# One buffer for the normalized tokens of two sublayers, and two more blocks counted in the first

## The chip, the core and the metric

The kernel runs on one core of a Trainium2 chip. The core has five engines with their own instruction queues: PE (matrix products; its weight loads are listed as PEld), DVE (vector), ACT (scalar functions and copies), POOL (here mostly indirect transfers) and SP (here only starts transfers). Each engine works through its own queue in order and waits on semaphores for the others. The metric is the device time of one execution in microseconds, and the median of several runs.

## The reference, cut to what matters

The program is a network of four layers on 1250 tokens of 512 numbers, with a graph of 21,250 edges. The change lies between the first layer's second half and the second layer's first half:

```python
# layer 0, second half: experts chosen with balanced gates
xn = _layernorm(x)
gates = clip(xn @ gate_w, 1e-10)          # 1250 x 8, then 8 rounds of balancing
#   each round: divide each column by its sum, then each row by its sum
# each of 8 experts takes its N // 8 = 156 tokens of largest gate; a taken token
# whose gate is above 0.5 gets tok @ experts[e], the others get zero from e;
# a token's result is the sum over its experts / (number of experts that took it + 1)
x = x + moe(xn)

# layer 1, first half: graph attention beside a global attention, same input
xn = _layernorm(x)
x = x + gat(xn, src, dst) + mix(xn)
#   mix: q, k, v = xn @ Wq.T, xn @ Wk.T, xn @ Wv.T ; softmax of q over features,
#        of k over tokens; (q (k^T v) + xn) @ W1.T @ W2.T + the same
#   gat: two dense-graph attention layers of 4 heads; needs, for every pair of
#        nodes, how many edges join them
```

The last comment is why the kernel has a table of counts: 1250 x 1250 numbers that say how often an edge runs from one node to another. It depends on the edges alone, so it can be made at any time before layer 1's graph attention.

## The kernel before, in words

**Tiles.** The tokens lie in 10 tiles of 128 rows (the last has 98). `self.x` holds them all. `norm_tile(t, out)` (lines 215 to 223) writes the normalized rows of tile t, from a mean and a variance that `row_stats` made (lines 201 to 208: two statistics instructions and a sum on DVE, a square root on ACT); if `ready(t)` has been called before, only a reciprocal (line 221) and one DVE instruction (line 222) are left. `transpose_tile` (line 156) turns a 128 x 512 tile with four PE instructions (line 160) into a PSUM bank and copies it out with `evac`, which takes ACT (line 134) and DVE (line 136) in turn. `layernorm` (line 225) does both for all ten tiles.

**Counting.** `count_blocks(blocks, signs)` (line 666) is a generator. The edges are sorted by target and cut into 12 blocks of 107 nodes, each of 16 tiles of 128 edges (the last has 12). For every tile of edges it makes a one-hot row (`ohs`, 128 x 1251), multiplies it on PE with the targets' one-hot (`ohb`, loaded by SP at line 688) in three products of 512, 512 and 227 columns (line 711), and yields. The three sums of a block take three banks of PSUM, named `more`, of which there are just three. At the block's end they are emptied, brought together (`acc`) and stored to the table (lines 712 to 726; the two stores of line 1096). With `signs` the rows are signs made by ACT (line 695), and, once `count_even` is set, every second one is made by DVE (line 692); the differences of neighbouring columns are then taken on DVE (line 720) after ACT has emptied the banks (line 719). Without `signs` DVE makes true one-hots (line 697) and ACT alone empties the banks (line 725). The 128 x 1251 row of column numbers, `wide`, is made by POOL (line 675), and `at`, the edges' numbers, by DVE (line 678), once for each use of the generator.

**Layer 0's second half**, `layer0_ffn` (line 1629), with the counting of the first six blocks mixed in by calls of `self.count(n)`, each of which draws n tiles of edges:

- norms and turns of the ten tiles, and the gate products (line 171, 8 columns each)
- 8 balancing rounds (lines 1651 to 1664), a chain of one PE product and seven short DVE instructions each, with one counted tile a round
- the top choice: 20 rounds of `max` and `match_replace` on DVE (lines 1679 and 1683), with two counted tiles a round
- places and slots (lines 1687 to 1732), which end in `putI`, the row that each token goes to, and `getI`, the row that it is fetched from; PE turns the slots at line 1707
- 20 scatters on POOL (line 239) of the normalized rows to the experts' input, then 24 counted tiles
- the scattered rows are loaded (`xr`, line 1744), turned (`rT`), multiplied with the eight experts' weights (line 179, 160 columns) and the results turned back and stored (lines 1756 and 1759)
- for each tile: two gathers on POOL (line 231), two sums into `x` on DVE (line 1787), the statistics, and two counted tiles

**Layer 1's first half**, `layer1_attn` (line 2164): it opens its own pools for the normalized tokens (`xn`, natural, and `xnT`, turned), for weights and for PSUM, calls `layernorm`, and then `global_attention` (line 1790), which is given a second use of the counting generator, for the other six blocks, as `steps`: every step draws four counted tiles, and there is one step after each of the 12 key products and after each of the 10 turns of the keys (line 1817), and so on until the blocks are done. Then `gat_dense` uses the table.

**What sets the order.** The program text gives an order, but a scheduler, working at build time from the dependencies and from an estimate of each instruction's time, decides where each instruction stands in its engine's queue. Buffers come from pools: when a pool is closed and another one takes its place, the new buffers wait for the last users of the old ones. The chip then runs the queues as they are.

The functions that the change touches:

## Time and profile before

| | us |
|---|---|
| median of 3 runs | 4508.17 |
| lowest and highest | 4505.29, 4512.73 |
| the profiled execution's own time | 4474.11 |
| its span, first to last instruction | 4472.3 |

The stretches of the profiled execution that the change touches, in microseconds from the span's start:

| stretch | from | to |
|---|---|---|
| layer 0: norms, turns, gate | 1573.9 | 1601.5 |
| balancing | 1601.5 | 1621.2 |
| top choice, up to the turn of the slots | 1621.2 | 1705.1 |
| scatters, up to the first turn of the scattered rows | 1705.1 | 1740.3 |
| experts | 1740.3 | 1788.5 |
| gathers and sums | 1788.5 | 1826.0 |
| layer 1: norms, first key products | 1826.0 | 1843.8 |
| keys and counting | 1843.8 | 1916.9 |

A profile is one execution. The page's first part gives each engine's busy time, its share of the span and its number of instructions. The table of stretches gives for each window: its length, then the busy time and the number of instructions for PE, PEld, DVE, ACT and POOL, then the clock that PE was granted (1.00 is full speed, 0.50 is half), the mean busy share of the transfer engines, and the GB/s that they moved. The timeline gives start, duration, engine, line, operation, what is written from what, shapes and a count, and in brackets how long the engine had been idle and what ended that. Neighbouring instructions of one kind are merged into one line. Products in 32-bit floats appear as two entries each in the timeline.

### The profile page before, as it was taken

The page shows a single profiled execution, that of the slowest core. Times are in us where ns is not written, and L with a number is a line of the kernel's source. Part 1 is how long each engine was busy: PE and PEld are TensorE (multiplying, and loading weights), DVE is VectorE, ACT ScalarE, POOL GpSimd, SP SyncE. Part 2 cuts the span into 40 slices and gives each one's busy share as a digit, 9 for nine tenths or more (in the row PEclk, how much of TensorE's full clock was granted, in tenths as well). Part 3 has the DMA queues.
Part 4 walks back from the last instruction along what each step waited for, and adds up shares of the span by engine and source line. Part 5 has one row for each costly group of instructions (what it writes and reads, how often), then busy time and mean ns, then how long its engine had stood idle before and what let it go on. Part 6 is the DMA issues. An engine that isn't in the chain of part 4 may idle for free.

```text
span 4472.3 us, 49493 instructions
## 1 busy us (share of the span) xinstructions
PE 3913.2 (87%) x15451; PEld 2422.1 (54%) x15466; DVE 2696.8 (60%) x6357; ACT 1598.2 (36%) x2955; POOL 1358.0 (30%) x1308
## 2 busy tenths in 40 slices
PE   6987998899888866799999999997979896898796
PEld 3444554555454445444788877564546562455474
DVE  5358894888499864633896768314484225687301
ACT  2222442334233373110464446223452232555121
POOL 2017773776477402202000000103131013675102
PEclk9989999999999978899999999999999998997798
DMA  6437664766466423402421110384002653666695
GB/s 220 159 82 220 200 196 146 208 197 192 147 198 184 128 69 108 124 14 64 147 70 40 49 35 29 143 289 137 12 27 76 225 198 122 179 204 203 226 338 187
DMA packets 283002, 647.59 MB, mean 145 GB/s; under 512 B 61673, under 2 KB 108905, under 8 KB 267322
## 3 DMA queue, kind: packets, MB, share of 16 engines
q1 hardware_dynamic: 169290, 357.13, 24.1%
q0 software_dynamic: 73088, 234.75, 18.2%
q10 hardware_dynamic: 40352, 52.44, 3.4%
q8 instruction: 127, 2.08, 0.2%
q14 instruction: 145, 1.19, 0.1%
HBM read 528.87 MB, written 120.65 MB: 145 GB/s over the span
## 4 chain that ended last, share of the span: by engine, by line
PE 31%; DVE 8%; DMA 5%; issue 4%; ACT 2%; POOL 2%; SPq 0%; POOLq 0%; ACTq 0%; DVEq 0%
PE more L2105 5%; PE mm L1968 4%; PE mm L179 3%; PE mm L171 3%; PE mm L3168 2%; PE mm L2357 2%; PE mm L2352 2%; PE more L2688 2%; DMA hs<-gcn_h,srcI 1%; PE mm L2688 1%; PE mm L2067 1%; DMA xe<-routed_in 1%; PE mm L776 1%; DVE junk L1996 1%; DVE e L2030 1%
## 5 line engine op out<-in xcount | busy, mean ns | idle before, releaser
L231 POOL DMA_INDIRECT xl<-xl,srcI x564 | 617.5, 1095 | 282.4 <-issue 134.6
L1353 PE MATMUL more<-xl,wT 128*128 128x512 f32 x1128 | 578.6, 600 | 13.5 <-ACT wT L1343 13.0
L1286 PE MATMUL mm<-hl,oh 121*128 121x512 f32 x564 | 418.1, 741 | 56.7 <-DVE s L1299 32.7
L1302 DVE SCALAR_TENSOR_TENSOR junk<-s,att 128x512 f32<-128x512 f32 x534 | 416.3, 780 | 6.8
L1299 DVE TENSOR_TENSOR s<-xl,mm 128x512 f32<-128x512 f32 x534 | 357.7, 679 | 79.0 <-PE mm L1287 64.4
L2105 PE MATMUL more<-hh,e 128*128 128x259 f32 x1600 | 383.7, 385 | 10.8 <-ACT o L2048 8.5
L2105 PEld LDWEIGHTS more<-hh,e 128*128 128x128 f32 x1600 | 295.1, 191 | 74.8 <-issue 16.0
L171 PE MATMUL mm<-w,xnT 128*128 128x512 f32 x640 | 306.0, 617 | 16.7 <-ACT xnT L2383 12.1
L231 POOL DMA_INDIRECT hs<-gcn_h,srcI x188 | 217.1, 1155 | 85.7 <-issue 24.9
L1353 PEld LDWEIGHTS more<-xl,wT 128*128 128x128 f32 x1128 | 195.7, 192 | 73.7 <-issue 27.8
L1287 PE MATMUL mm<-hl,oh 121*128 121x512 f32 x564 | 234.1, 415 | 0.0
L231 POOL DMA_INDIRECT g<-routed_out,getI x60 | 67.3, 1122 | 486.7 <-DMA routed_out<-o 414.9
L1286 PEld LDWEIGHTS mm<-hl,oh 121*128 121x128 f32 x564 | 110.4, 196 | 191.1 <-issue 89.2
L2025 ACT ACTIVATE e<-r,hh 128x512 f32<-128x512 f32 (+1 forms) x240 | 154.3, 646 | 132.3 <-PE more L2105 121.3
L171 PEld LDWEIGHTS mm<-w,xnT 128*128 128x128 f32 x640 | 122.9, 197 | 143.7 <-issue 124.6
L3006 PE MATMUL more<-hl,oh 128*128 128x512 f32 x376 | 160.8, 529 | 27.0 <-DVE oh L2970 11.6
L1273 ACT ACTIVATE oh<-nb 112x512 fp32r<-112x512 bf16 x141 | 88.7, 630 | 266.4 <-DMA nb<-nbt 197.4
L2028 ACT ACTIVATE e<-r,a 128x512 f32<-128x512 f32 (+1 forms) x240 | 152.3, 646 | 68.8 <-DVE e L2030 56.7
L1166 PE MATMUL tab<-w,xT 128*128 128x512 f32 x320 | 166.2, 614 | 8.9 <-ACT xT L1415 6.1
L2030 DVE TENSOR_TENSOR e<-e,e 128x512 f32<-128x512 f32 (+1 forms) x240 | 141.9, 597 | 51.6 <-ACT e L2025 45.3
L1287 PEld LDWEIGHTS mm<-hl,oh 121*128 121x128 f32 x564 | 111.1, 197 | 111.1 <-issue 109.5
L2966 ACT ACTIVATE hl<-hs,rec 128x512 fp32r<-128x512 f32 x188 | 131.0, 717 | 98.2 <-DMA hs<-gcn_h,srcI 45.7
(631 smaller groups left out, 7783.3 us busy)
## 6 DMA issues: line engine op xcount, KB each, us to landing
w<-L_ffn_Wp SPq DMA_DIRECT2D x64, 1024.0 KB
w<-L_ffn_table SPq DMA_DIRECT2D x56, 1025.0 KB
neg<-ntab SPq DMA_DIRECT2D x80, 320.0 KB
nb<-nbt SPq DMA_DIRECT2D x141, 128.0 KB
hl<-xr SPq DMA_DIRECT2D x36, 448.0 KB
xr<-tro SPq DMA_DIRECT2D x30, 512.0 KB
xe<-routed_in SPq DMA_DIRECT2D x56, 256.0 KB
routed_out<-o ACTq DMA_DIRECT2D x56, 256.0 KB
```

The source lines that it names most:

```text
L171: self.nc.tensor.matmul(p, lhsT=xT[:, c, t * 128:(t + 1) * 128], rhs=w[:, c, n0:n0 + n], start=c == 0, stop=c == k - 1)
L231: self.nc.gpsimd.indirect_dma_start(out=out, out_offset=None, in_=table, in_offset=bass.IndirectOffsetOnAxis(ap=idx, axis=0), bounds_check ...
L1166: nc.tensor.matmul(d[name], lhsT=xT(c), rhs=L[name][:, c, :], start=c == 0, stop=c == 3)
L1286: nc.tensor.matmul(m, lhsT=s, rhs=hl[:K, 0, :], start=True, stop=False)
L1287: nc.tensor.matmul(m, lhsT=s, rhs=hl[:K, 1, :], start=False, stop=not on_pe(i))
L1299: nc.vector.tensor_tensor(o, d["xl"][:, j, :D], s, op=ALU.add)
L1302: nc.vector.scalar_tensor_tensor(junk, s, 0.0, L["att"], op0=ALU.max, op1=ALU.mult, accum_out=d["lg"][:, j:j + 1])
L1353: nc.tensor.matmul(B[b]["y"], lhsT=d["wT"][:, j, :], rhs=d["xl"][:, j, :D], start=k == 0 and j == 0, stop=last and j == GE - 1)
L1968: nc.tensor.matmul(m, lhsT=chunk(layer, c)[:, t * 128:(t + 1) * 128], rhs=w[:, c, :], start=c == 0, stop=c == k - 1)
L2030: nc.vector.tensor_tensor(e1[:, :n], e1[:, :n], e2[:, :n], op=ALU.max)
L2105: nc.tensor.matmul(ys[j], lhsT=e[:, j * 128:(j + 1) * 128], rhs=HH[q][:, s, :], start=s == 0, stop=s == NT - 1)
L3006: nc.tensor.matmul(y, lhsT=oh, rhs=hl[:, i], start=i + j == 0 and not (self.fast and k), stop=last and i + j == GE)
```

## The change: what it does

- `CB`, the number of blocks counted with signs in layer 0, goes from 6 to 8; the second use of the generator counts the other 4.
- One function, `layer0_ffn_to_layer1_attn`, replaces the lines in `run` and `layer1_attn`. It opens one `xnT`, one `xn`, one pool of weights and one set of PSUM banks for both halves, and passes `xn` and `xnT` to `layer0_ffn`.
- In `layer0_ffn` each of layer 0's ten norm tiles draws one counted tile; the 24 after the scatters become 56; and in the gather loop each tile, as soon as its sums and statistics are done, is normalized and turned for layer 1 into the same `xn` and `xnT`, with one counted tile instead of two. The pool of short-lived tiles moves to the other side of the memory.
- What is left of the first eight blocks is drawn after `layer0_ffn`; then the counting buffers are closed and opened again for the second use, and `global_attention` follows without a `layernorm` of its own.

```diff
-CB = 6
+CB = 8
@@ run
-            self.count_ctx = ExitStack()
-            with self.weights():
-                self.count_pool = self.count_ctx.enter_context(
-                    self.tc.tile_pool(name="count", bufs=1, side="right"))
-                self.ctab = self.dram.tile([NP, NP], F16 if fast else F32, name="ctab")
-                self.counting = self.count_blocks(range(CB), True) if fast else iter(())
-                with self.psum(3, 2, 3) if fast else self.psum():
-                    self.layer0_ffn()
-                    for _ in self.counting:
-                        pass
-            self.count_ctx.close()
-            self.count_pool = self.count_ctx.enter_context(
-                self.tc.tile_pool(name="count", bufs=1, side="right"))
-            self.layer1_attn()
+            self.layer0_ffn_to_layer1_attn()
@@
+    def layer0_ffn_to_layer1_attn(self):
+        fast = self.fast
+        count_ctx = ExitStack()
+        def count_pool():
+            self.count_pool = count_ctx.enter_context(
+                self.tc.tile_pool(name="count", bufs=1, side="right"))
+        self.ctab = self.dram.tile([NP, NP], F16 if fast else F32, name="ctab")
+        with self.tc.tile_pool(name="l1a", bufs=1) as p:
+            xnT = p.tile([128, 4, NP], F32, name="xnT")
+            with self.tc.tile_pool(name="l1b", bufs=1) as pb:
+                xn = pb.tile([128, NT, D], F32, name="xn")
+                with self.weights(), self.psum(3, 2, 3) if fast else self.psum():
+                    count_pool()
+                    self.counting = self.count_blocks(range(CB), True) if fast else iter(())
+                    self.layer0_ffn(xn, xnT)
+                    self.count(NB * 16)
+                    count_ctx.close()
+                    count_pool()
+                    if fast:
+                        steps = islice(self.count_blocks(range(CB, NB), False), 3, None, 4)
+                    else:
+                        steps = self.count_steps()
+                    self.global_attention(xn, xnT, steps)
+                    for _ in steps:
+                        pass
+            count_ctx.close()
+            with self.psum(2, 2, 4), self.tc.tile_pool(name="l1g", bufs=1, side="right") as pg:
+                self.gat_dense(xnT, pg)
@@ layer0_ffn
-    def layer0_ffn(self):
+    def layer0_ffn(self, xn, xnT):
...
-                self.tc.tile_pool(name="l0ft", bufs=2) as tmp:
+                self.tc.tile_pool(name="l0ft", bufs=2, side="right") as tmp:
...
-            xn = p.tile([128, NT, D], F32, name="xn")
-            xnT = p.tile([128, 4, NP], F32, name="xnT")
-            self.layernorm(xn, xnT)
+            for t in range(NT):
+                self.norm_tile(t, xn[:, t, :])
+                self.transpose_tile(xnT[:, :, t * 128:(t + 1) * 128], xn[:, t, :])
+                self.count(1)
...
-            self.count(24)
+            self.count(56)
...
                 self.ready(t)
-                self.count(2)
+                self.norm_tile(t, xn[:, t, :])
+                self.transpose_tile(xnT[:, :, t * 128:(t + 1) * 128], xn[:, t, :])
+                self.count(1)
@@
-    def layer1_attn(self):
...
```

More of the change, by code (lines that the diff above doesn't have):

```diff
@@ L2162, in gat_dense @@
                 step[0] += 1
-    def layer1_attn(self):
-        nc, I = self.nc, self.I
-        with self.tc.tile_pool(name="l1a", bufs=1) as p:
-            xnT = p.tile([128, 4, NP], F32, name="xnT")
-            with self.weights(), self.psum(3, 2, 3) if self.fast else self.psum():
-                with self.tc.tile_pool(name="l1b", bufs=1) as pb:
-                    xn = pb.tile([128, NT, D], F32, name="xn")
-                    self.layernorm(xn, xnT)
-                    if self.fast:
-                        steps = islice(self.count_blocks(range(CB, NB), False), 3, None, 4)
-                    else:
-                        steps = self.count_steps()
-                    self.global_attention(xn, xnT, steps)
-                for _ in steps:
-                    pass
-            self.count_ctx.close()
-            with self.psum(2, 2, 4), self.tc.tile_pool(name="l1g", bufs=1, side="right") as pg:
-                self.gat_dense(xnT, pg)
     def top2(self, p, v):
```

## The prediction

> **What bounds the kernel now.** I read the page first, then one table of engine times over the eight stretches that the change touches, the same table for the counting products alone (line 711), and the timeline around the joints. The program is a series of stages, each with its own limit, so the 87% for PE says little:
>
> ```profile
> span 4472.3 us, 49493 instructions
> ...
> PE 3913.2 (87%) x15451; PEld 2422.1 (54%) x15466; DVE 2696.8 (60%) x6357; ACT 1598.2 (36%) x2955; POOL 1358.0 (30%) x1308
> ```
>
> The stretches, in order: norms and gate; balancing; top choice; scatter; experts; gathers; layer 1's norms; layer 1's keys and the turning of the keys.
>
> ```profile
> core 0: us, PE busy (x) PEld busy (x) DVE busy (x) ACT busy (x) POOL busy (x), PEclk, DMA share, GB/s
> 1573.90:1601.50 27.60, 26.49 (x122) 25.27 (x123) 10.11 (x31) 9.46 (x11) 1.00 (x1) 0.50 0.45 166
> 1601.50:1621.20 19.70, 12.25 (x51) 6.20 (x52) 12.43 (x57) 15.23 (x12) 0.00 (x0) 0.83 0.06 20
> 1621.20:1705.10 83.90, 52.16 (x198) 21.87 (x202) 80.28 (x95) 69.78 (x65) 0.00 (x0) 0.85 0.13 37
> 1705.10:1740.30 35.20, 14.64 (x67) 7.11 (x67) 11.38 (x32) 12.60 (x14) 22.68 (x21) 0.69 0.24 71
> 1740.30:1788.50 48.20, 46.84 (x336) 44.80 (x336) 12.11 (x26) 10.44 (x26) 0.00 (x0) 0.95 0.53 178
> 1788.50:1826.00 37.50, 7.68 (x41) 4.09 (x42) 27.38 (x58) 1.74 (x9) 23.06 (x20) 0.64 0.72 164
> 1826.00:1843.80 17.80, 15.89 (x56) 10.58 (x57) 11.33 (x34) 3.34 (x7) 0.00 (x0) 0.70 0.64 237
> 1843.80:1916.90 73.10, 72.08 (x336) 40.20 (x342) 48.07 (x97) 19.33 (x35) 0.00 (x0) 1.00 0.21 64
> ```
>
> PE is full in the first stretch, at half clock; DVE is full in the third; in the fourth PE is idle for 20.6 of 35.2 us while POOL issues 20 scatters; in the sixth it is idle for 29.8 us under the gathers; in the last it is full at full clock. So a counting product is free in the scatter stretch and costs its whole time in the last. The counting alone:
>
> ```profile
> 1573.90:1601.50 27.60, 0.99 (x2) 0.47 (x3) 0.50 0.45 166
> ...
> 1705.10:1740.30 35.20, 13.49 (x57) 5.98 (x57) 0.69 0.24 71
> ...
> 1843.80:1916.90 73.10, 42.68 (x215) 21.64 (x222) 1.00 0.21 64
> ```
>
> The timeline gives prices and joints:
>
> ```profile
> 1598.58 0.59 PE L711 MATMUL more<-ohs,ohb 128*128 128x512 bf16 x1
> 1599.39 0.40 PE L711 MATMUL more<-ohs,ohb 128*128 128x227 bf16 x1 [0.22 <-issue]
> 1740.32 1.97 PE L160 MATMUL tp<-ident,xr 128*128 128x128 f32 x8 [20.06 <-DMA xr<-l0moe_in]
> 1825.21 0.73 DVE L1787 SCALAR_TENSOR_TENSOR x<-g,G,x 98x512 f32<-98x512 f32 x1
> 1845.73 0.42 DVE L136 COPY big<-mm 128x256 f32<-128x256 f32 x1 [4.47 <-PE mm L179]
> 1868.58 2.28 PE L711 MATMUL more<-ohs,ohb 128*128 128x512 bf16 x12
> ```
>
> A counted tile is three products: 1598.58 to 1599.79 is 1.2 us at half clock; twelve in 2.28 us is 0.57 us a tile at full clock. PE waits 20 us for the scattered rows. The last sum of layer 0 ends at 1825.9; PE's first 256-column key product starts at 1843.8, so 17.9 us lie between.
>
> [...] The trace agrees for the norms (turns and 8-column gate products, half clock from 1573.9 until 1608), less so after 1740.3, where turns alone took the clock up within 5 us. [...] here a scatter took 2.12 us beside a subtraction of line 720 and mostly 0.98 without. [...]
>
> **The change part by part.** The order of instructions in the changed program, as built, tells where each counted tile goes on PE (before, then after): norms and gate 1, 11; balancing 12, 12.3; top choice up to the slots' turn 64, 62.3; scatter 19, 38.3; between experts and layer 1's norms 14, 4; from there to the first 256-column key product 0, 8; afterwards 78, 52. The total is 188 in both.
>
> 1. *Norms and gate, ten tiles more.* PE is full, so each is on the path. If the clock stays at half: 10 x 1.2 = 12 us. But the new order begins with 7 turns, a tile, a turn, a tile, 4 turns: over 5 us without a gap, mostly wide products, which should release the clock. At full clock the same work is cheaper: 8 turns take 1.97 us at half and 1.04 to 1.13 at full (1837.8, 1767.0); a weight load is 0.216 us against 0.137 (40 in 8.66 at 1590, 16 in 2.20 at 1750), so the 80 gate products fall from 17.1 to about 11. If the first 6 us are slow and the rest fast: 28 turns 3.7 + gate 11 + 9 tiles 5.1 = 19.8, ending at 1599.8. ACT, which makes the one-hots (1.24 to 1.34 us each, 11 and five copies of 0.59: some 18 us), is covered. Ends: -2 and +12. I take 0, because three wide products a tile are what the old stretch lacked. SP issues three ohb loads ahead of gw (some 1.7 us later); gw is now first read behind two tiles, which covers it.
>
> 2. *Balancing to the slots.* DVE is a serial chain here. One subtraction L720 (1.44) moves into the fifth balancing round, between lines 1662 and 1663; from there to putI there are 5 of them instead of 4, and 12 L692 in both: +1.4. The first three rounds took 2.63 us against 2.36 for the others; with the clock up before them -0.8. Sum +0.7; ends +0.3 and +2.5.
>
> 3. *Scatter.* 38.3 tiles instead of 19. Those 19 ran from 1706.3 to 1720.3: 5 tiles at half clock in 5.0 us, the rest at about 0.61 (one-hots by ACT and DVE in turn), and a stop while ACT empties the banks. For 36.6 tiles before the first turn of the scattered rows: 5 x 1 + 31.6 x 0.61 + 2 stops x 2.4 = 29 us, against 34 that PE has: hidden. On SP, xr's loads stand behind the seventh block's two stores and four ohb loads; that block ends at about 1725, the scatters at 1736.5. Without the cover each tile would cost 0.6. Ten more L692 and 1.7 tiles among xr's turns: +1; ends 0 and +6.
>
> 4. *Experts to gathers.* The four mix weights (1 MB each) move on SP from 1826 to where experts 4 to 7 leave their buffers (about 1769 to 1787). The last lies beside the last two output stores (0.25 MB each, 1788.4), for which the first gather waits: at the 390 GB/s that such loads reached at 1580 a megabyte is 2.7 us. I take +1; ends 0 and +3. In return PE doesn't wait for the key weights. The eighth block's last four tiles replace 14 behind the experts; both lie under the wait for the gathers.
>
> 5. *Norms among the gathers.* Removed: the norms, turns and copies in the 17.9 us after the last sum. Added per tile on DVE, beside 2 x 0.75 + 0.68 + 0.17 + 0.15: reciprocal 0.15, norm 0.54, half a copy 0.35. That is 3.5 us by durations, about 3.0 by spacing (two sums stood 0.67 apart at 1808.5). With four one-hots of 0.54, at's 0.33 and a copy, DVE needs 33 to 38 us; POOL needed 1796.3 - 1825.9 = 29.6 for the loop and gains the iota L675 (1.2 + 0.3) behind the 11th gather, which nine gathers queue behind. So the last norm ends at 1831 to 1834 instead of about 1837.5; then four turns (1.0), one product and four tiles (3.1 at full clock, 6.7 at half), and the 256-column product starts at about 1838.3: -5.5; ends -9 and 0.
>
> 6. *Layer 1.* 26 tiles fewer in a stretch where PE is full: 26 x 0.57 = -14.8. The cover of the exponential's chain (4.7 tiles at the first turns of the keys) is in the new order too, and the turns without a tile beside them now stand among the products of line 1827. I take -14.5; ends -15 and -12.
>
> Sum: 0 + 0.7 + 1 + 1 - 5.5 - 14.5 = -17.3 us. The profiled execution took 4474.1 (span 4472.3); changed, 4456.8. The runs' median is 4508.2, 34 above it; the same difference gives 4490.9. Later stages are the same instructions in the same order and shift whole.
>
> **The rivals.**
> *The norms stay at half clock* (for: turns and gate products kept it there for 34 us; against: the gapless start). Term 1 is +12, the sum -5.3: 4502.9.
> *DVE becomes the bound under the gathers* (for: 27.4 of 37.5 us busy already; against: the spacing). Term 5 is 0, the sum -11.8: 4496.4.
> *Slower: the clock stays at half in the norms and in the scatter stretch too.* Then 36.6 tiles at 1.25 with two stops are 50.5 us in 35.2: +15 in term 3, +12 in term 1; sum about +10: 4518. It decides once a scatter tile averages above 0.93 us (34 / 36.6) and the norms gain nothing; each tenth above is 3.7 us. Against: the clock was up from 1711.7 while tiles followed each other.
> *The change doesn't do what it says:* excluded for the order (norms stand among the sums, tiles moved); possible only as waits that keep PE standing.
>
> **How the numbers follow.** My forecast, 4491: 0.57, its own range 4482 to 4499. Cold norms, 4503: 0.22. DVE-bound gathers, 4496: 0.12. Slower, 4518: 0.09. A measurement of this kernel tells 0.2%, 9 us, from no change: faster is below 4499. The forecast gives nearly all of its share, the gathers most of theirs, cold norms a tenth: faster 0.66. Slower (above 4517) is half of its rival and a little for unseen waits, 0.07; same 0.27. For 8 in 10 the range goes from 4480 (term 5 at -9, term 4 at 0, term 1 at -2, term 6 at -15, so a sum near -26) to 4512 (cold norms, and half of the scatter's overrun).
>
> **What would show it.** First balancing product no later than 1602, with a clock above 0.5 in the norms (term 1); the scattered rows' first turn still about 35 us behind the slots' turns, PE idle just before it (3); the last x sum within 33 us of the first gather's landing, and the key products some 12 us behind it (5); counting in the key stretch down by a third and the stretch still full (6). It is wrong if the norms stretch by 10 us, if xr's loads are issued late, or if gathers come more than 1.7 us apart.

## The result and the profile after

The changed kernel takes 4489.8 us (median of 13 runs, 4480.1 to 4503.5) against 4503.7 for the kernel before in runs alongside (13 runs, 4487.6 to 4515.1): ratio 0.997, 95% interval 0.9956 to 0.9984. That is faster by 13.9 us between the medians, or 0.3%; the forecast was 17.3 us less, and 4491 for the time itself.

The profiled execution of the changed kernel took 4489.8 us, with this span and these totals on its page:

```profile
span 4487.9 us, 49486 instructions
...
PE 3922.2 (87%) x15466; PEld 2415.7 (54%) x15466; DVE 2689.5 (60%) x6338; ACT 1622.8 (36%) x2976; POOL 1351.0 (30%) x1308
```

This span is 15.6 us longer than the one profiled before, although the kernel is faster. The profile tells why that is no contradiction: the first turn of layer 0's norms comes 21.4 us later (1573.9 before, 1595.3 after), in stages that the change doesn't touch, and from the end of layer 1's products of P (those of line 1827, which follow the keys) to the end of the span it is 2518.7 us before and 2527.1 after, unchanged instructions again. Between these two points, where the change lies, it is 379.7 us before and 365.5 after: 14.2 less, which agrees with the medians. All that follows is therefore measured between such anchors inside one trace, not from the start of the span.

The table of engine times over the stretches, in the order and with the columns of the one shown before (norms and gate; balancing; top choice; scatter; experts; gathers; from the last sum to the first 256-column key product; keys):

```profile
core 0: us, PE busy (x) PEld busy (x) DVE busy (x) ACT busy (x) POOL busy (x), PEclk, DMA share, GB/s
1595.30:1618.00 22.70, 21.90 (x153) 17.50 (x153) 10.50 (x31) 20.12 (x21) 1.01 (x1) 0.85 0.60 208
1618.00:1637.70 19.70, 13.27 (x53) 6.72 (x53) 12.46 (x54) 15.97 (x16) 0.00 (x0) 0.74 0.12 35
1637.70:1722.30 84.60, 52.07 (x201) 21.46 (x198) 80.93 (x100) 71.38 (x66) 0.00 (x0) 0.81 0.13 38
1722.30:1762.10 39.80, 28.51 (x120) 13.41 (x121) 15.33 (x39) 24.89 (x24) 20.59 (x20) 0.75 0.28 86
1762.10:1809.50 47.40, 46.49 (x347) 44.17 (x346) 12.96 (x28) 12.78 (x28) 0.00 (x0) 1.00 0.73 235
1809.50:1853.40 43.90, 13.58 (x48) 7.39 (x46) 29.37 (x70) 4.42 (x14) 22.18 (x21) 0.62 0.75 170
1853.40:1864.90 11.50, 10.82 (x44) 5.30 (x42) 8.02 (x22) 2.06 (x5) 0.00 (x0) 0.80 0.05 13
1864.90:1938.00 73.10, 72.38 (x306) 38.71 (x305) 37.62 (x74) 17.42 (x31) 0.00 (x0) 1.00 0.16 50
```

The first row is the surprise: with ten tiles more PE is through five us sooner, at a mean clock of 0.85 instead of 0.50. The scatter row is 4.6 us longer than before, the gather row 6.4 us longer, and the row behind the last sum, 17.8 before, is 11.5. The counting products alone, in the norms, the scatter stage and the keys:

```profile
1595.30:1618.00 22.70, 8.72 (x33) 3.66 (x33) 0.85 0.60 208
1722.30:1762.10 39.80, 27.35 (x110) 12.18 (x110) 0.75 0.28 86
1864.90:1938.00 73.10, 30.91 (x158) 15.21 (x156) 1.00 0.16 50
```

The tiles are where the order said: 11 in the norms, 36.7 before the scattered rows' first turn, and 158 products instead of 215 in a key stretch that is still full.

Term by term, in us between the same anchors. Term 1 runs from the first norm turn to the first balancing product, 2 on to the slots' turns, 3 on to the first turn of the scattered rows, "experts" to their last turn, 4 on to the first gather, then some four us to the first x sum; 5 from there to the first 256-column key product, 6 on to the end of P's products. w1_pool, explained below, differs from the changed kernel in the queue of one load, which lies at the same place in time, and serves as a second look at it.

| term | before | changed | forecast of the difference | measured | w1_pool | measured |
|---|---|---|---|---|---|---|
| 1 norms and gate | 27.67 | 22.76 | 0 | -4.9 | 22.54 | -5.1 |
| 2 balancing to slots | 103.55 | 104.21 | +0.7 | +0.7 | 102.60 | -1.0 |
| 3 slots to scattered rows | 35.20 | 39.86 | +1 | +4.7 | 36.00 | +0.8 |
| experts | 47.67 | 46.67 | 0 | -1.0 | 48.65 | +1.0 |
| 4 experts to first gather | 4.21 | 7.02 | +1 | +2.8 | 10.52 | +6.3 |
| 5 first x sum to 256-column product | 47.54 | 44.99 | -5.5 | -2.6 | 45.22 | -2.3 |
| 6 keys to the end of P | 109.78 | 95.95 | -14.5 | -13.8 | 95.95 | -13.8 |
| all, with first gather to first sum | 379.68 | 365.53 | -17.3 | -14.2 | 365.28 | -14.4 |

The total is near the forecast because term 1, five us better than forecast, and terms 3 to 5, in sum eight us worse in either profile, were off in opposite directions. The experiments ask why.

### The profile page after: what moved, and what is told of

The parts are those of the page before. It is cut to its first block, busy times and chain, and to the rows that moved or that the text cites. A ratio compares the mean times of both kernels' runs of the same rounds, so it can differ in the third digit from the quotient of the medians.

```text
span 4487.9 us, 49486 instructions
## 1 busy us (share of the span) xinstructions
PE 3922.2 (87%) x15466; PEld 2415.7 (54%) x15466; DVE 2689.5 (60%) x6338; ACT 1622.8 (36%) x2976; POOL 1351.0 (30%) x1308
## 5 line engine op out<-in xcount | busy, mean ns | idle before, releaser
L1353 PE MATMUL more<-xl,wT 128*128 128x512 f32 x1128 | 579.7, 601 | 14.5 <-ACT wT L1343 14.0
L2129 PEld LDWEIGHTS more<-hh,e 128*128 128x128 f32 x1600 | 295.1, 191 | 75.8 <-issue 17.8
L711 PE MATMUL more<-ohs,ohb 128*128 128x512 bf16 x564 | 137.5, 383 | 42.8 <-ACT ohs L695 18.0
```

The lines of the kernel that those rows point to most:

```text
L1353: nc.tensor.matmul(B[b]["y"], lhsT=d["wT"][:, j, :], rhs=d["xl"][:, j, :D], start=k == 0 and j == 0, stop=last and j == GE - 1)
L2129: nc.tensor.matmul(ys[j], lhsT=e[:, j * 128:(j + 1) * 128], rhs=HH[q][:, s, :], start=s == 0, stop=s == NT - 1)
```

## The experiments

Twelve kernels were run. Times of the stretches are from each one's own trace, one execution each, between the same anchors; ratios are to the kernel before, run alongside. The ratios alone say little about single causes: the interval of every one of the twelve except struct6 overlaps the changed kernel's, so what follows rests on the traces, and on how far they agree with each other.

**norms_bare: what brings the clock up.**

```diff
             for t in range(NT):
                 self.norm_tile(t, xn[:, t, :])
                 self.transpose_tile(xnT[:, :, t * 128:(t + 1) * 128], xn[:, t, :])
-                self.count(1)
             gw = pg.tile([128, 4, 8], F32, name="gw")
```

> The changed kernel without the counted tile per normalized tile in layer 0's norms; ten tiles come later instead (four among the gathers, six behind them), nothing is left out. Clock theory: the tiles are what brings TensorE's clock up, so the norms and the gate, 22.8 us in the changed kernel, go back to 27 to 28 us at a granted clock near 0.5, although PE has ten tiles (30 products) less to do there; about 4.5 us longer. Rival, work alone: the clock would rise anyway, and the stretch gets shorter by ten tiles of 0.57 to 1.2 us, to 11 to 17 us. Behind the gathers six tiles of 0.57 us: 0 to 3.4 us longer. Whole kernel: theory 4 to 8 us slower than the changed one, 0.998 to 0.999 of before; rival 3 to 8 us faster.

Norms and gate took 27.68 us, against 27.67 in the kernel before; ratio 0.9978 (0.9967 to 0.9989). The same windows, the first six us and the rest, of the changed kernel and then of norms_bare:

```profile
1595.30:1601.30 6.00, 5.39 (x20) 3.44 (x21) 5.42 (x11) 4.79 (x6) 1.01 (x1) 0.50 0.88 289
1601.30:1618.00 16.70, 16.51 (x134) 14.06 (x134) 5.08 (x20) 15.33 (x16) 0.00 (x0) 0.98 0.50 179
```

```profile
1581.40:1587.40 6.00, 5.30 (x23) 4.50 (x24) 5.71 (x11) 1.37 (x3) 0.98 (x1) 0.50 0.94 303
1587.40:1609.00 21.60, 21.41 (x101) 20.76 (x101) 4.39 (x20) 8.08 (x8) 0.00 (x0) 0.50 0.34 128
```

Both begin equally busy (5.39 and 5.30 of 6 us). Then the changed kernel runs at 0.98 and norms_bare, 99% busy for 21.6 us, stays at 0.50. The clock theory holds, the rival of mere work falls by more than 10 us. The other traces agree: in all eleven that have tiles in the norms the recorded clock rises 5.2 to 7.3 us after the first turn, and in the three without them (the kernel before, norms_bare, struct6) it stays at 0.50 until the norms are over. Behind the last sum norms_bare has only one tile more than the changed kernel, the others stand mostly under the wait for the gathers, and terms 5 and 6 together took 139.85 against 140.94: there the tiles cost nothing.

**scat40: fewer tiles behind the scatters.**

```diff
             self.count_even = True
-            self.count(56)
+            self.count(40)
```

> The changed kernel with 40 counted tiles asked for behind the scatters instead of 56: sixteen tiles come later (four among the gathers, twelve behind them). Theory: the scattered rows' first turn was 4.7 us late because it stands behind 36.6 counted tiles on PE, which ran at 1.3 us a tile from the ninth us of the scatters on; with 16 fewer it starts 35.2 us behind the slots' turns again (39.9 in the changed kernel), and PE idles before it. Twelve tiles more behind the gathers cost 12 x 0.57 = 6.8 us, so the end comes 1 to 3 us later than in the changed kernel. Rival, the scatters or the loads of the scattered rows themselves are late: the first turn stays 39 to 40 us behind the slots, and the end comes 6 to 7 us later.

The first turn of the scattered rows came 36.15 us behind the slots' turns, ratio 0.997 (0.9958 to 0.9982). That looks like the theory, but it is a poor test: most of the tiles that were to leave run in the stage all the same (35.0 before that turn instead of 36.7), and kernels that leave the stage untouched gave the same: w1_pool 36.00, norms_behind 35.59, gated4 35.97. So the 39.9 of the changed kernel's profile is nothing that its order always brings. The counting in the scatter stage (PE alone), in the changed kernel's profile and then in w1_pool's:

```profile
1733.86 4.99 PE L711 MATMUL more<-ohs,ohb 128*128 128x512 bf16 x24 [0.69 <-ACT ohs L695]
1740.52 1.22 PE L711 MATMUL more<-ohs,ohb 128*128 128x512 bf16 x6 [1.67 <-issue]
1743.11 1.26 PE L711 MATMUL more<-ohs,ohb 128*128 128x512 bf16 x6 [1.37 <-ACT ohs L695]
1745.97 2.25 PE L711 MATMUL more<-ohs,ohb 128*128 128x512 bf16 x6 [1.60 <-ACT ohs L695]
1752.97 2.40 PE L711 MATMUL more<-ohs,ohb 128*128 128x512 bf16 x6 [4.75 <-issue]
1756.07 6.24 PE L711 MATMUL more<-ohs,ohb 128*128 128x512 bf16 x25 [0.69 <-ACT ohs L695]
1762.14 0.60 PE L160 MATMUL tp<-ident,xr 128*128 128x128 f32 x4
```

```profile
1723.12 8.59 PE L711 MATMUL more<-ohs,ohb 128*128 128x512 bf16 x42 [0.69 <-ACT ohs L695]
1732.19 1.27 PE L711 MATMUL more<-ohs,ohb 128*128 128x512 bf16 x6 [0.49 <-ACT half L719]
1734.15 5.29 PE L711 MATMUL more<-ohs,ohb 128*128 128x512 bf16 x25 [0.69 <-ACT ohs L695]
1748.36 1.11 PE L160 MATMUL tp<-ident,xr 128*128 128x128 f32 x4 [8.93 <-DMA xr<-l0moe_in]
```

In w1_pool the fourteen tiles of a block follow each other in 8.59 us (0.61 a tile, as the prediction had it), all are done at 1739.4, and PE idles for 8.9 us until the scattered rows land: the stage is hidden. In the changed kernel's profile the same tiles come in pairs with 1.4 to 4.8 us between them. There PE and the makers of one-hots wait for each other: ACT's and DVE's next one-hot starts when a signal from PE comes in, and these signals arrive 1 to 7 us behind the modelled end of the product they tell of (0.04 to 0.6 us in w1_pool). What is known of that is taken up at the end.

**w1_pool: one weight load on another queue.**

```diff
-            w1 = self.weight(I["L1_mix_W1"], 4, D)
+            w1 = self.weight(I["L1_mix_W1"], 4, D, nc.gpsimd)
```

> The changed kernel with one of the four mix weights (L1_mix_W1, 1 MB) loaded from POOL's queue, behind the gathers, instead of SP's queue beside layer 0's last two output stores. Theory: those stores took 5.1 and 5.3 us to land beside that load, 2.0 and 2.3 us in the kernel before, and the first gather waits for them; with the load gone from there they land in 2 to 2.5 us and the first gather starts 4.2 us behind the experts' last turn instead of 7.0. Rival, the eighth block's store to ctab is what the first gather waits for: it stays near 7 us. Another: POOL's own issue of the load delays a gather or the iota, and the x sums take 2 us longer. Whole: theory 2 to 3 us less than the changed kernel up to the end of the products of L1827's kind; rivals 0 or 2 more.

The first gather came 10.52 us behind the experts' last turn, not 4.2; ratio 0.9965 (0.9951 to 0.9978). The edit didn't do what it was to do: in the built order POOL issues the load ahead of the gathers, which wait, at 1796.3, and so beside the last two output stores (1797.4 and 1797.9) as before. These landed after 8.0 and 8.4 us, no sooner than with all four loads on SP (5.1 to 7.9 us in six traces with four buffers). Who issues the load brought nothing here. The question of term 4 stayed open until gated4.

**norms_behind: the norms out of the gather loop.**

```diff
                 self.ready(t)
-                self.norm_tile(t, xn[:, t, :])
-                self.transpose_tile(xnT[:, :, t * 128:(t + 1) * 128], xn[:, t, :])
                 self.count(1)
+            self.layernorm(xn, xnT)
             g1.close()
```

> The changed kernel with layer 1's norms and turns behind the whole gather loop again instead of tile by tile in it; buffers still shared, eight blocks, same counts. Theory, the norms among the gathers bring 2.6 us because DVE, slower in the loop, gives back half: from the first x sum to the first 256-column key product 47 to 48 us instead of 45.0; the x sums alone take about 30 us again instead of 33.5, and some 17 us follow. Rival one, the whole gain of that stretch is from the key weights being there early and the tiles moved, not the norms: 45 us or less. Rival two, predicted before: the norms among the gathers bring 5.5 us: 50 us or more.

From the first x sum to the first 256-column product it took 52.0 us, which was written down for rival two; ratio 0.9981 (0.9973 to 0.9989). So the norms among the gathers are worth 52.0 - 45.0 = 7.0 us, and not 2.6. The reason that the changed kernel shows only 2.6 of it against the kernel before is the tiles: eight counted tiles stand behind the last sum in the changed kernel and in norms_behind, none in the kernel before, and 47.5 + 8 x 0.57 = 52.1. The stretch behind the last sum of norms_behind, then the rest up to the end of P:

```profile
1837.20:1859.16 21.96, 19.90 (x80) 12.54 (x81) 14.73 (x42) 3.92 (x8) 0.00 (x0) 0.76 0.02 7
1859.16:1955.12 95.96, 95.23 (x359) 48.87 (x358) 38.34 (x75) 17.99 (x32) 0.00 (x0) 1.00 0.13 38
```

**struct6 and count8: the two halves of the change alone.** struct6 is the changed kernel with the old counting:

```diff
-CB = 8
+CB = 6
...
                 self.transpose_tile(xnT[:, :, t * 128:(t + 1) * 128], xn[:, t, :])
-                self.count(1)
             gw = pg.tile([128, 4, 8], F32, name="gw")
...
-            self.count(56)
+            self.count(24)
...
                 self.transpose_tile(xnT[:, :, t * 128:(t + 1) * 128], xn[:, t, :])
-                self.count(1)
+                self.count(2)
             g1.close()
```

> The shared buffers and the norms among the gathers alone: six blocks in layer 0 and the counts asked for as in the kernel before (none in the norms, 24 behind the scatters, two a tile in the gathers). Theory, the gain is the counting's and the structure only pays for itself: norms and gate 26 to 28 us at half clock again; the first gather some 9.5 us behind the experts' last turn (4.2 before), because the mix weights' loads lie beside the output stores; from the first x sum to the end of the products of P some 150 us, against 157.3 before and 141 in the changed kernel; in sum about 2 us less than before, ratio 0.999 to 1.001. Rival, the structure brings the larger part: 10 us or more less than before, ratio 0.998 or lower.

count8 is the kernel before with the new counting:

```diff
-CB = 6
+CB = 8
...
-            self.layernorm(xn, xnT)
+            for t in range(NT):
+                self.norm_tile(t, xn[:, t, :])
+                self.transpose_tile(xnT[:, :, t * 128:(t + 1) * 128], xn[:, t, :])
+                self.count(1)
...
-            self.count(24)
+            self.count(56)
...
                 self.ready(t)
-                self.count(2)
+                self.count(1)
```

> The counting alone: the kernel before (own buffers, layer 1's norms behind the gathers) with eight blocks in layer 0 and the changed kernel's counts (one a tile in the norms, 56 behind the scatters, one a tile in the gathers). Theory: norms and gate 22 to 23 us; the scattered rows' first turn 35 to 37 us behind the slots' turns; the first gather 4 to 5 us behind the experts, since no mix weight is loaded beside the stores; from the first x sum to the end of P's products 157.3 less 26 x 0.57 = 142 to 143 us; in sum 18 to 20 us less than before, 3 to 6 less than the changed kernel, ratio 0.995 to 0.997. Rival, the norms among the gathers are needed for it (their 7 us): ratio 0.998 or higher, behind the changed kernel.

| us | before | struct6 | count8 | changed |
|---|---|---|---|---|
| 1 norms and gate | 27.67 | 27.68 | 23.12 | 22.76 |
| 3 slots to scattered rows | 35.20 | 35.16 | 35.91 | 39.86 |
| 4 experts to first gather | 4.21 | 8.55 | 4.14 | 7.02 |
| 5 + 6 first x sum to the end of P | 157.32 | 151.07 | 146.85 | 140.94 |
| whole stretch | 379.68 | 377.15 | 367.52 | 365.53 |
| ratio | | 1.0003 (0.9993 to 1.0012) | 0.9961 (0.9948 to 0.9973) | 0.997 (0.9956 to 0.9984) |

struct6 fits its theory: the norms among the gathers save 6.3 us in terms 5 and 6 and the late gather takes 4.3 back. count8 did better than its rival and, in its trace, less well than its theory: 12.2 us less rather than 18 to 20. Terms 5 and 6 fell by 10.5 instead of 14.8 (eight of the 26 tiles come back behind the last sum: 18 x 0.57 = 10.3), and the experts and the wait for the first sum together took 2.6 us more than before, which no run explains. In its row behind the last sum, 17.8 us before, PE is busy for 19.6 of 21.7 us:

```profile
1822.21:1843.90 21.69, 19.62 (x79) 12.29 (x81) 14.68 (x43) 3.92 (x8) 0.00 (x0) 0.77 0.57 200
```

The counting is the change's gain, by the runs too: struct6's interval holds 1, count8's does not. The two halves together (12.2 + 2.5 = 14.7) give what the changed kernel has (14.2), so neither needs the other.

**gated4: no load beside the last stores.**

```diff
+        if after is not None:
+            self.nc.scalar.copy(w[0:1, 0, 0:1], self.x[0:1, after, 0:1])
         self.nc.sync.dma_start(w, src.rearrange("(k p) n -> p k n", p=128))
...
-            wk = self.weight(I["L1_mix_WkT"], 4, D)
+            wk = self.weight(I["L1_mix_WkT"], 4, D, after=0)
```

and likewise for WvT (2), WqT (4) and W1 (6).

> The changed kernel in which each of the four mix weights' loads waits for an x sum (tiles 0, 2, 4 and 6), by a copy of one element of x into the weight's tile on ACT ahead of the load; nothing else differs. Theory: the loads beside layer 0's last output stores are what makes the first gather late (7 to 10.5 us behind the experts' last turn in the runs of the changed structure, 4.2 before); with none of them there the last stores land in 2.0 to 2.5 us and the gather starts 4 to 5 us behind. The loads then lie beside the gathers: the x sums take 0 to 4 us longer than 33.5. In sum 2 to 5 us less than the changed kernel up to the end of P's products. Rival one, the block's store to ctab or the shared pool holds the gather: it stays above 7. Rival two, the megabytes cost the gathers what they cost the stores: the gather earlier, the sums as much later, in sum 0.

The last stores, issued at 1785.8 and 1786.2, landed after 2.0 and 2.3 us, and the first gather came 4.16 us behind the experts; ratio 0.9953 (0.9936 to 0.9969). The queues around the first gather (POOL, SP and ACT's issues alone) in the changed kernel, then in gated4:

```profile
1807.80 0.37 SPq L141 DMA_DIRECT2D w<-L_mix_W  x1
1809.24 0.81 ACTq L1781 DMA_DIRECT2D l0moe_out<-o  x2
1813.51 0.77 SPq L1096 DMA_DIRECT2D ctab<-acc  x2
1815.83 1.05 POOL L231 DMA_INDIRECT g<-l0moe_out,getI  x1 [62.05 <-DMA ctab<-acc]
```

```profile
1785.76 0.81 ACTq L1783 DMA_DIRECT2D l0moe_out<-o  x2
1789.48 1.44 POOL L233 DMA_INDIRECT g<-l0moe_out,getI  x1 [56.42 <-issue]
1790.03 0.81 SPq L1098 DMA_DIRECT2D ctab<-acc  x2
```

In the changed kernel the loads are just ahead of the stores and the gather stands 6.6 us behind their issue; the trace's landing signals have the second store landing at 1814.94, 0.9 us before the gather. The label names the store to ctab only because that wait is the last of several by the profile: its own second half landed at 1816.06, after the gather had begun, and in gated4 it is issued behind the gather. The theory of the late gather holds, and rival one fell. Rival two is largely right as well: the four megabytes now lie beside the gathers, which follow each other every 1.58 us instead of 1.42, and the x sums take 36.2 us instead of 33.5 (1.41 to 1.52 us and 32.5 to 34.9 us in the other traces with the norms among the gathers and at most eight blocks). From the experts' last turn to the end of P it is 154.3 us, against 152.0 in the changed kernel's profile and 155.1 and 155.5 in scat40 and w1_pool. The bytes have to pass somewhere, and by these traces both places cost about the same.

**steps_later: is it the order on DVE?** Behind the last sum, the last norm (L222) stands on DVE behind three one-hots and a copy that wait for PE.

```diff
                     self.evac(kT[:, f, s:s + n], self.feat(wk, xnT, f, s, n))
-                    next(steps, None)
+                    f and next(steps, None)
```

> The changed kernel without the counting behind the first three key products (twelve tiles are drained later, nothing is left out). Theory: layer 1's last norm is late because it stands on DVE behind three one-hots and a copy that wait for PE; with fewer of them it ends 2 to 3 us earlier behind the last x sum (6.96 us in the changed kernel), and from the last x sum to the first 256-column key product it takes 5 to 7 us instead of 11.5, of which the eight tiles that leave are 4.6; those and four more come back later at 0.57 us a tile, so from the first x sum to the end of P's products 2 to 3 us less than the 141 of the changed kernel. Rival, PE is the bound there and the order on DVE costs nothing: the same 141 us.

The stretch behind the last sum fell to 8.6 us, not to the 5 to 7 written down, and term 6 rose from 95.95 to 98.70: from the first x sum to the end of P 141.7 us, against 140.9. The last norm did end 2.6 us earlier behind the last sum, as the theory had it, and nothing was gained by it. The rival is right: in the changed kernel PE is busy for 10.82 of those 11.50 us, so the order on DVE costs nothing; ratio 0.9954 (0.9937 to 0.9970).

**w5: a fifth weight buffer.**

```diff
-                with self.weights(), self.psum(3, 2, 3) if fast else self.psum():
+                with self.weights(5), self.psum(3, 2, 3) if fast else self.psum():
```

> The changed kernel with five weight buffers instead of four in the shared scope: each load of the experts' and of the mix weights is issued one expert (4.8 us) earlier, so that the fourth megabyte of the mix has landed or nearly so when the last two output stores are issued. Theory, a load beside these stores is what delays the first gather: with the last load some 4.8 us earlier they land in 2 to 4 us, the first gather starts 4 to 6.5 us behind the experts' last turn (7 to 10.5 in the changed structure, 4.2 with the loads held back), and the gathers are not slowed as they were with the loads held back: from the experts' last turn to the end of P's products 150 to 152 us, against 155 (mean of three runs of the changed order) and 154.3 (held back). Rival, the queue is behind by more than a load: the gather stays at 8 us or more and the stretch at 155.

The first gather came 8.87 us behind the experts, ratio 0.997 (0.9958 to 0.9983). The loads did move an expert ahead, but a fifth, L1_mix_W2T, moved into the place that had become free (issued at 1807.6, the stores at 1809.1 and 1809.5). From the experts' last turn to the end of P it took 156.6 us. Both are what the rival said: one buffer more brought one load more.

**w5_keys and w5_c9: work for PE under the gathers.** Both with five buffers. The first orders the key products by column slice:

```diff
-            for f in range(4):
-                for s, n in SLICES:
+            for s, n in SLICES[:-1]:
+                for f in range(4):
                     self.evac(kT[:, f, s:s + n], self.feat(wk, xnT, f, s, n))
                     next(steps, None)
+            for f in range(4):
+                for s, n in SLICES[-1:]:
+                    self.evac(kT[:, f, s:s + n], self.feat(wk, xnT, f, s, n))
+                    next(steps, None)
```

> As with five weight buffers, and the key products ordered by column slice (all four feature blocks of the first two slices, then the four 256-column ones) instead of by feature block. Theory, behind the last x sum PE is the bound (10.8 busy of 11.5 us) while under the gathers it is idle for 30 of 44 us; four to six more of the 512-column slices (1.9 us each) can run there: from the first x sum to the end of P's products 5 to 10 us less than 141. Rival, the reductions and exponentials, now all at the end, become the bound: PE stands 4 to 8 us ahead of the first turned key and the sum is 140 to 146.

From the first x sum to the end of P 131.7 us, 9.2 less than the changed kernel and 11.0 less than w5, from which it differs by this order alone; ratio 0.9954 (0.9939 to 0.9968). From the experts' last turn to the last sum, to the first 256-column product, and to the end of P:

```profile
1805.71:1852.08 46.37, 19.01 (x65) 9.98 (x63) 29.45 (x71) 5.10 (x15) 22.81 (x21) 0.67 0.76 165
1852.08:1888.45 36.37, 36.37 (x151) 17.86 (x149) 22.01 (x49) 5.11 (x12) 0.00 (x0) 1.00 0.12 34
1888.45:1950.34 61.89, 61.27 (x239) 33.20 (x238) 24.28 (x47) 14.84 (x26) 0.00 (x0) 1.00 0.08 25
```

Under the gathers PE does 19.0 us of work, against 14.3 in the changed kernel, and from the last sum on it is full at full clock, where the changed kernel's row has 0.80; it is idle for only 0.6 of the last 61.9 us, so the rival fell. PE's busy time over the three stretches is 3.7 us less as well (116.65 against 120.32), which the clock can explain but no run separates. The second counts a ninth block under the gathers:

```diff
-CB = 8
+CB = 9
...
+            self.count_even = False
             oT = xnT
...
                 self.transpose_tile(xnT[:, :, t * 128:(t + 1) * 128], xn[:, t, :])
-                self.count(1)
+                self.count(3)
             g1.close()
```

> As with five weight buffers, and nine blocks counted in layer 0, three tiles a round in the gather loop with all their one-hots made on ACT (idle there for 39 of 44 us). Theory, counting under the gathers is free while ACT has room (22 tiles of 1.24 us are 27 us): the sixteen tiles that leave the stretch behind are worth 16 x 0.57 = 9 us, less 1.5 us of DVE for one more block: 5 to 8 us less from the first x sum to the end of P's products than 141. Rival, DVE and the DMA queues are full there (one more block's subtraction, ohb loads beside the gathers): the x sums take 3 us or more longer, and less than half of it is left.

First x sum to the end of P 138.4 us, 2.6 less than the changed kernel and 4.3 less than w5, with x sums of 35.6 us; ratio 0.9962 (0.9947 to 0.9976). Against w5 the gain falls short of the theory's lower end, against the changed kernel it is half of it; the x sums are 2.1 us longer than in the changed kernel, less than the rival's 3.

**combined.**

```diff
-CB = 8
+CB = 9
```

with three tiles a round under the gathers, the key products by column slice as above, four buffers, and the loads of WqT and W1 held back as in gated4, for the sums of tiles 1 and 5 (they went out at 1841.3 and 1841.8, ahead of the last gather only).

> The changed kernel with what the earlier runs spoke for: key products by column slice, nine blocks in layer 0 with three tiles a round under the gathers (their one-hots on ACT alone), and the loads of the last two of the four prefetched mix weights (L1_mix_WqT and L1_mix_W1) held back until the x sums of tiles 1 and 5; four weight buffers as before. If the parts add: the keys 9 us and the ninth block 2.5 us less than the changed order in the stretch from the first x sum to the end of P's products (141 to about 129), the first gather 4.2 to 6.5 us behind the experts' last turn instead of 7 to 10.5, gathers slowed by 1 to 3 us by the two loads; from the first norm turn to the end of P's products 351 to 354 us against 379.7 before and 365 in the changed order, ratio to before 0.9935 to 0.9945. Rival, keys, norms, one-hots' block and sums share DVE under the gathers and don't add: 356 us or more, ratio 0.9950 or higher.

First norm turn to the end of P: 354.4 us, 25.3 less than before and 11.1 less than the changed kernel, just above the 351 to 354 written down and below the rival's 356; ratio 0.9952 (0.9934 to 0.9970), an interval that holds both. The first gather is at 4.01 us. Keys and ninth block don't add up: first x sum to the end of P is 134.9, against 131.7 for the keys with eight blocks. By its trace it is ahead of both kernels; by the runs it is ahead of the kernel before by its whole interval, while its interval and the changed kernel's overlap. Nor do the runs rank the variants as the traces do: gated4 and steps_later, whose traces lie within 1.7 us of the changed kernel's, have the same ratio (0.9953 and 0.9954) as w5_keys and combined, 9 and 11 us ahead by theirs. So the gain of the last two over the changed kernel is shown by one trace each, not by the times.

## Why the prediction was right, and where it was not

The forecast of 4491 and its sign were right; that the time came within 1.2 us is luck twice over: the difference was 13.9 us and not 17.3 (the kernel before ran at 4503.7 alongside, not at 4508.2), and it came that near only because term 1 and terms 3 to 5 were off by five and by eight us in opposite directions. What was right as mechanism and size is the counting moved out of the full stretch, term 6.

1. *Norms and gate, forecast 0, measured -4.9: outside its ends.* The mechanism was right in the main: the start with wide products releases the clock, 6.6 us after the first turn, and norms_bare shows that without them it isn't released. That the start has no gap, on which the step's estimate also counted, is not what does it: norms_bare runs without one from 1584.3 on and stays at 0.50. The prices of the rest were too high. After the release the changed kernel's 28 turns take 3.1 us (3.7 priced), the gate products' entries (two to a product) 110 ns each (137 priced, from weight loads of another stage; at half clock they take 211), so 78 in 8.6 us, and the tiles 4.6 (5.1): 16.3 us instead of 19.8. The working also gave -1.9 (6 + 19.8 against 27.7), and 0 was taken all the same.
2. *Balancing to the slots:* +0.7 forecast and measured in the changed kernel's own profile; -1.0 to +0.7 in the others. Right within what such a stretch varies.
3. *Scatter stage: right in most traces.* +1 forecast; +0.4 to +1.5 in nine of the eleven traces that have the new counts there, with PE idle for 5.4 to 10.8 us before the scattered rows in all nine, and 0.71 to 0.82 us a tile with the stops (29 us for 36.6, or 0.79, was priced). The +4.7 of the changed kernel's own profile and 42.8 us in w5_c9 are the exceptions; in both PE's signals came late, of which more at the end.
4. *Experts to gathers, forecast +1 with ends 0 and +3: too small.* The step named the right cause, a megabyte beside the last two stores, and priced it at the time of that megabyte alone. The stores landed after 5.1 to 8.4 us instead of 2.0 to 2.3, since the loads follow each other every 4.8 us from expert 4 on and the last isn't always the only one in flight (in w1_pool WqT, issued at 1791.2, landed at 1798.7, after the stores' issue). In the changed kernel it was +2.8, in nine other kernels with the loads there +3.3 to +6.3; in count8, gated4 and combined, without them, it was -0.2 to 0.
5. *Norms among the gathers, forecast -5.5, measured -2.6, within its ends.* The norms brought 7.0 us. The step that failed is the last: it put one product and four tiles behind the last norm, and eight tiles had to run there on a PE that was full (4.6 us, 2.3 of them priced). The last x sum ended 33.5 us behind the first instead of the 29.6 that POOL's loop had needed, and the last norm 40.5 us behind it rather than 35 to 38, but steps_later shows that the norm's lateness cost nothing. That DVE would bind under the gathers was half right: the last sum ends 4.5 us behind the last gather's landing (1848.9), against 1.0 us before.
6. *Keys: right.* -13.8 for 26 tiles fewer, 0.53 a tile; 0.57 was priced.

Of the rivals, the cold norms fell with the first row of the table, and norms_bare shows that they were only one line of code away. With them fell the slower case. Its other half, a tile above 0.93 us in the scatter stage, did come in the changed kernel's own profile (36.7 tiles in 38.7 us before the turn), with PE waiting between pairs of tiles, and in nine of the eleven traces it didn't. Of the three signs that would make it wrong one came, in the changed kernel's profile: the loads of the scattered rows were issued 3.4 us behind the last scatter instead of 1.1, since SP stood behind the seventh block's store. These 2.3 us are about half of the 4.7; the rest is PE's, whose counted tiles ran until the turn. Both come from the late counting, since the store waits for the block's end.

## What to carry to other kernels

Price work added to a full engine at the clock that it will itself bring about: here ten tiles made a stretch five us shorter. When a scope is shared, look at what its queue now issues early and which small transfer it lies beside: the four prefetched megabytes held the first gather back by 3 to 6 us through two stores of a quarter megabyte, and in gated4 cost about as much beside the gathers. And count products behind the last wait: what an engine can't do under the wait it does after it, so by the traces the order of the products (9 us in w5_keys) was worth more than the order of the norms (7 us).

## What the runs showed of the hardware that was not expected

*Being recorded busy was not enough for the clock.* In the trace of the kernel before 95 of 96 recorded stretches of one clock, and in the changed kernel's 107 of 108, are a whole number of 3.41 us long; the odd one is the last of each. In norms_bare PE is recorded busy for 21.41 of 21.60 us, with 74 entries of 8-column products, 24 turns and one counted tile, and the granted clock is 0.50 throughout; with eleven tiles of wide products among the same turns and gate products it was 0.98 from the seventh us on. In one stretch turns brought it up by themselves: in the kernel before the clock rises from 0.50 to 1.00 at 1744.7, and in the 3.41 us ahead of that PE is recorded busy for only 2.81 us, with nothing but turns until the first product after them starts at 1744.6. So in these traces the share of time that PE is recorded busy doesn't tell whether the clock will rise. That the products of 8 columns kept it down is an inference from these two stretches; no run takes them out alone, and how long the array itself works on such a product no run shows, as the trace's ends of products are modelled.

*PE's signals came late in five traces.* A one-hot has four buffers, so a new one waits for the last product of the fourth tile back. In nine traces it starts within 0.6 us of that product's modelled end, as long as tiles follow each other. In the changed kernel's own the delay grows from 1.0 us at 15 us behind the slots' turns to 7.3 at 32 us, in w5_c9 to 9.7, each time with a signal of PE recorded 0.02 to 0.4 us ahead of the start, and the counting falls from 0.61 to some 1.4 us a tile. In w5, w5_keys and combined the same begins only at 23 to 25 us and reaches 3.6 to 5.1 us; there the stage still hid it (36.7, 36.6 and 36.2 us). These five are also the traces with an incomplete record: between the first and the last scatter they have 2.7 to 4.4 landing signals for each DMA, against 15.1 to 15.9 in the nine others, and in the stage 57 to 71 of some 85 signals of PE, where the nine have all. And they are the five that reach the first norm turn latest, at 1591.0 to 1598.5 us against 1572.3 to 1587.2. So the late signals go with these executions and not with the kernel: the changed order has them in some traces and not in others. Whether they belong to the chip in those executions or to the recording of them wasn't tried and stays open; the 4.7 us of term 3, and perhaps the 21 us by which the changed kernel's profile starts its norms later, can't be put down to the change.
